# Two steps per pair for the causal convolution that is made ahead, held in place on VectorE

## The chip, the cores and the metric

The kernel runs on one core of a Trainium2 chip. The metric is the device time of one execution in microseconds (us), lower is better. Everything is float32.

## The reference, cut to what matters

A tensor `x` of 4 sequences (b) x 512 time steps (t) x 128 x 64 features passes through two layers.

Layer 0, for each sequence: a layer norm, three projections to 64 states, a decaying scan over time and a projection back ("attention"); a layer norm and a 3-tap convolution over the frequency axis with a gelu; a layer norm and a **causal depthwise convolution over time** with 3 taps, followed by another layer norm; and a feed-forward block of 64 to 256 to 64 features with a gelu. Each part is added to the residual. The part that is changed is this one:

```python
xn = layernorm(x.reshape(b, t, d), ln_time_g, ln_time_b)
to = conv_general_dilated(swap(xn), time_W, (1,), [(2, 0)], feature_group_count=d)
to = layernorm(swap(to + time_b), time_ln_g, time_ln_b)
x = x + to.reshape(b, t, f, h)
```

Layer 1 splits off a moving average over time, mixes the lowest 128 Fourier modes of the rest with complex weights, transforms back and adds the average.

## The kernel before, in words

Layer 0 holds a sequence as 64 chunks of 128 features x 512 times; two chunks are a **pair**, so that most tiles are 128 x 2 x 512. A sequence goes through five stages, each a Python generator that issues its instructions and yields after every small step: `project` (J), `scan` (Z), `attend_and_convolve` (A), `convolve_time` (C), `open_feed` (O) and `feed_forward` (F). `in_turn` runs two sequences against each other: a list of stage pairs with weights says which generator makes the next step. In two of these stretches F of sequence b (0, then 1) runs beside J and Z of sequence b+2.

The order of the instructions on TensorE is the order in which the program issues them (`manual_schedule`). On VectorE, ScalarE, GpSimd (POOL) and the DMA queue of SyncE (SP) a scheduler sorts them when the kernel is built, by program order and by when it takes them to be ready, so an instruction whose inputs are there early can be placed far ahead of its place in the program. `tc.keep_in_program_order(ins)` adds an edge from the last instruction that the program gave to the same engine: `ins` is issued after that one. It sets no upper end.

**Feed-forward** steps through c = 0 to 65. Step c issues `widen(c, 0)` and `widen(c, 1)` (four matmuls of L656 into PSUM tiles `m` and `c`, each followed by a gelu on ScalarE, L660); for odd c `add_residual` (two ScalarE instructions, L633, themselves held in program order, and the VectorE sum L636), for even c `residual` (two loads and the VectorE instructions L624 and L625); `narrow(c-1)` (eight matmul records of L667 into the single PSUM tile `p`, then the VectorE instruction L672, which empties it into `x4t`); and `store(c-2)` (four transposes, ScalarE copies, and for each fourth chunk a store of 1 MB on POOL's queue, L692). One step of `project` follows: two matmul pairs of L360, and for each pair of chunks two loads into a tile `wx` (two buffers), two VectorE scalings (L357) and two statistics (L344).

**The causal convolution** of a pair is in `taps`: a load of the pair (L555), two VectorE instructions that normalize it (L556, L557), two on ScalarE that make the first tap (L560), four on VectorE that add the other taps (L564), a correction of two columns on POOL (L568) and a store of the result to DRAM on POOL's queue (L569). `convolve_time` does this for all 32 pairs of a sequence. For sequences 1 and 2 the first 12 pairs (`AHEAD`) are made ahead by the generator `convolve_ahead`, from inside `feed_forward` of the sequence before, on tiles `x1` (three buffers) and `z` (four); `convolve_time` later fetches these results. `convolve_ahead` first spreads two rows of statistics over the partitions with matmuls into `p` (L240, copied by L284), in two calls, and then makes one pair per call. `feed_forward` calls it at the head of each step with c % 4 == 3: the rows at c = 3 and 7, the pairs at c = 11 to 55.

Of the kernel before, what the change touches and what calls it, by code (L numbers as in the profile page):

```python
# [12 lines left out]
ALU = mybir.AluOpType  # L13
# [9 lines left out]
SL = 512  # L23
# [56 lines left out]
def layer0(ctx, tc, dram, x, xt, vecs, wkvr, wo, wdec, wconv, fbias, w1, fb1, w2, fb2, x4):  # L80
# [4 lines left out]
    nc = tc.nc  # L85
# [464 lines left out]
        return t  # L550


    def taps(b, i, x2, xr, to, rb, mb):

        nc.sync.dma_start(x2, x2d[b][2 * i : 2 * i + 2].rearrange("c p t -> p c t"))  # L555
        nc.vector.tensor_tensor(xr, x2, pair_of(rb), ALU.mult)  # L556
        nc.vector.tensor_tensor(xr, xr, pair_of(mb), ALU.subtract)  # L557
        for j in range(2):
            c = slice(2 * i + j, 2 * i + j + 1)
            nc.scalar.activation(  # L560
                to[:, j, :], xr[:, j, :], AF.Identity, bias=tb_all[:, c], scale=vec[:, W2, c]
            )
            for k, w in ((1, W1), (2, W0)):
                nc.vector.scalar_tensor_tensor(  # L564
                    to[:, j, k:], xr[:, j, : SL - k], vec[:, w, c], to[:, j, k:], ALU.mult, ALU.add
                )
        cc = slice(2 * i, 2 * i + 2)
        nc.gpsimd.tensor_tensor(to[:, :, 0:2], to[:, :, 0:2], fix[:, cc, :], ALU.add)  # L568
        nc.gpsimd.dma_start(tod[b][cc].rearrange("c p t -> p c t"), to)  # L569

    def convolve_ahead(b):


        rb, mb = yield from rows(of_p, *carried[b], "rm3")
        ahead[b] = rb, mb
        for i in range(AHEAD):
            xr = spare("x1", SL)
            taps(b, i, xr, xr, spare("z", SL), rb, mb)
            yield

    def convolve_time(b):
        bank = of_a if b == B - 1 else of_p
        made = AHEAD if b in ahead else 0
        moment = carried.pop(b)
        if made:
            rb, mb = ahead.pop(b)
        else:
            rb, mb = yield from rows(bank, *moment, "rm" if b == B - 1 else "rm3")
        st = bank()
        waiting, added = [], 0  # L590
        n = NPR - made
        for k in range(n + 2):
            while waiting and waiting[0][0] == k - 2:
                add_up(st, 0, *waiting.pop(0)[1:], added == 0, added == NPR - 1)
                added += 1
            if k < n:
                if b == B - 1:

                    x2, xr, to, sq = spare("xp", SL), spare("x1", SL), spare("z", SL), two(bk, "sq")
                else:  # L600
                    x2 = bk.tile([P, 2, SL], F32, tag="kx", name="x2", bufs=3)
                    xr, to = two(bk, "kd"), bk.tile([P, 2, SL], F32, tag="k3", name="to", bufs=3)
                    sq = bk.tile([P, 2, SL], F32, tag="sq4", name="sq4", bufs=2)
                taps(b, made + k, x2, xr, to, rb, mb)
                nc.scalar.activation(sq, to, AF.Square)
                waiting.append((k, to, sq))
                i = k * made // n
                if i != (k + 1) * made // n:

                    to = fetch("kh", tod, b, i)  # L610
                    sq = bk.tile([P, 2, SL], F32, tag="mid", name="sq5", bufs=4)
                    nc.scalar.activation(sq, to, AF.Square)
                    waiting.append((k, to, sq))
            yield 7.0 * (NPR + 2) / (n + 2)
        mean, sq = yield from finish(st, bank, 4)
        causal[b] = moments(mean, sq, 4)
# [30 lines left out]
    def feed_forward(b):  # L647
        x3s = opened.pop(b)
        mids, x4s, obs = {}, {}, {}

        def widen(c, m):
            x3 = x3s[c // 2][:, c % 2, :]
            pm = c_bank() if m else two(ps_m, "m")
            for h in range(2):
                hs = slice(h * H, (h + 1) * H)
                nc.tensor.matmul(  # L656
                    pm[:, h, :], lhsT=w1_sb[hs, m * P : (m + 1) * P], rhs=x3[hs, :], start=True, stop=True
                )
            mid = mids[c, m] = bk.tile([P, 2, SL], F32, tag="mid", name="mid", bufs=4)
            nc.scalar.activation(mid, pm, AF.Gelu_apprx_tanh, bias=fb1_sb[:, m : m + 1])  # L660

        def narrow(c):
            pa = ps_p.tile([P, SL], F32, tag="p", name="pa")
            for m in range(2):
                mid = mids.pop((c, m))
                for h in range(2):
                    nc.tensor.matmul(  # L667
                        pa[h * H : (h + 1) * H, :], lhsT=w2_sb[:, m, :], rhs=mid[:, h, :],
                        start=(m == 0), stop=(m == 1),
                    )  # L670
            x4t = x4s[c] = bk.tile([P, SL], F32, tag="x4t", name="x4t", bufs=3)
            nc.vector.scalar_tensor_tensor(x4t, pa, fb2_sb, x3s[c // 2][:, c % 2, :], ALU.add, ALU.add)  # L672
            if c % 2:
                x3s.pop(c // 2)

        def store(c):
            x4t = x4s.pop(c)
            pool, tag = (ps_s, "s") if free_s[0] else (ps_p, "p")
            pt = pool.tile([P, NT, P], F32, tag=tag, name="pt")
            for t in range(NT):  # L680
                nc.tensor.transpose(pt[:, t, :], x4t[:, t * P : (t + 1) * P], ident)  # L681
            s = c // 4
            if c % 4 == 0:
                obs[s] = bk.tile([P, NT, SL], F32, tag="ob", name="ob")
            o = obs[s][:, :, c % 4 * P : (c % 4 + 1) * P]
            if c // 2 % 2:
                for h in range(2):
                    nc.scalar.copy(o[:, :, halves[1 - h]], pt[:, :, halves[h]])  # L688
            else:
                nc.scalar.copy(o, pt)  # L690
            if c % 4 == 3:
                nc.gpsimd.dma_start(  # L692
                    x4[b][:, s * SL : (s + 1) * SL].rearrange("(t p) d -> p t d", p=P), obs.pop(s)
                )

        early = None
        for c in range(NCH + 2):
            if b + 2 < B and c % 4 == 3:
                early = early or convolve_ahead(b + 1)
                next(early, None)  # L700
            if c < NCH:
                widen(c, 0)
                widen(c, 1)
            i = c // 2 + 2
            if i < NPR:
                if c % 2:
                    x3s[i] = add_residual(b, i, *coming)
                else:
                    coming = residual(b, i)
            if 0 < c <= NCH:  # L710
                narrow(c - 1)
            if c > 1:
                store(c - 2)
            yield 4.5


# [358 lines left out]
```

## Time and profile before

| what | value |
|---|---|
| median of 3 runs | 3868.74 us (3863.71 to 3873.1) |
| the profiled execution: its own time | 3868.33 us |
| the profiled execution: its span | 3866.3 us |
| TensorE (PE) busy, of the span | 3643.1 us, 94% |
| VectorE (DVE) busy | 2695.6 us, 70% |
| ScalarE (ACT) busy | 1722.6 us, 45% |
| POOL busy | 567.9 us, 15% |
| mean DMA rate | 236 GB/s |
| causal taps, L564, on tiles `z` | 224 instructions, 744 ns each (median) |

The span runs from the first to the last instruction on the core; the run's own time is 2.0 us longer. A line such as "ACT xf L871 <- PE a L867: 234.1, 64, 27.0" in a list of waits says that ScalarE stood idle ahead of L871 for 234.1 us in 64 waits, at most 27.0 us, until TensorE's L867 had finished. In a timeline a line has the start, the length, the engine, the program line, the operation and, in brackets, how long the engine was idle before it and what ended that.

The two stretches with F beside J and Z lie at about 830 to 1255 us and 1525 to 1955 us of the span.

### The profile page before, as it was taken

To read this page: it belongs to the slowest core of one execution; us is meant where nothing else is said; L and a number is where in the kernel's file an instruction comes from. 1 tells how busy PE (TensorE), PEld (TensorE's weight loads), DVE (VectorE), ACT (ScalarE), POOL (GpSimd) and SP (SyncE) were. 2 spreads that over 40 slices of the span, in tenths; PEclk is the share of its full clock that TensorE was granted. 3 is DMA by queue.
4 is the path that set the end of the run, shared out by engine and by line. 5 is a ranking of instruction groups with operands and counts; after the bars stand their busy time and mean duration, and the time that the engine had idled before them with its cause. 6 is when DMAs were issued, how large, how long until landed. Compare 5 with 4: busy or idle time off the path is not lost. (4 is left out here: it accounts for less than half of the span.)

```text
span 3866.3 us, 44881 instructions
## 1 busy us (share of the span) xinstructions
PE 3643.1 (94%) x15945; PEld 1343.5 (35%) x15945; DVE 2695.6 (70%) x3498; ACT 1722.6 (45%) x2427; POOL 567.9 (15%) x910
## 2 busy tenths in 40 slices
PE   9999999988999999899999988999989999999999
PEld 4433322233333223333322322333322843326533
DVE  4445669978656896865689799855558267792577
ACT  0023346645556564555656578867742210022100
POOL 0000012211000121110012121100025101141011
PEclk9999999999999999999999999999989999999999
DMA  9767657777765787776568677645559468994587
GB/s 310 262 215 251 222 181 260 258 242 273 255 229 183 235 279 259 248 257 231 191 229 274 215 252 248 213 162 179 182 192 289 145 217 293 314 295 157 191 299 266
DMA packets 432695, 913.86 MB, mean 236 GB/s; under 512 B 36248, under 2 KB 86616, under 8 KB 428376
## 3 DMA queue, kind: packets, MB, share of 16 engines
q1 hardware_dynamic: 350080, 634.55, 49.3%
q0 software_dynamic: 79872, 274.77, 20.3%
q8 instruction: 127, 2.08, 0.2%
q10 hardware_dynamic: 2520, 1.67, 0.1%
q14 instruction: 96, 0.79, 0.1%
HBM read 642.35 MB, written 268.50 MB: 236 GB/s over the span
## 5 line engine op out<-in xcount | busy, mean ns | idle before, releaser
L667 PE MATMUL pa<-mid,w_sb 128*64 128x512 f32 x2048 | 505.9, 615 | 74.0 <-DVE x4t L672 73.5
L660 ACT ACTIVATE mid<-m,fb_sb 128x1024 f32<-128x1024 f32 x256 | 284.5, 1111 | 245.0 <-PE m L656 244.5
L672 DVE SCALAR_TENSOR_TENSOR x4t<-pa,fb_sb,x 128x512 f32<-128x512 f32 x252 | 187.7, 745 | 200.5 <-PE pa L667 200.5
L656 PE MATMUL m<-x,w_sb 64*128 64x512 f32 x1008 | 291.7, 651 | 1.0 <-ACT mid L660 0.7
L660 ACT ACTIVATE mid<-c,fb_sb 128x1024 f32<-128x1024 f32 x256 | 283.0, 1106 | 1.2 <-PE c L656 1.1
L667 PEld LDWEIGHTS pa<-mid,w_sb 128*64 128x64 f32 x2048 | 126.3, 138 | 421.3 <-issue 223.8
L656 PE MATMUL c<-x,w_sb 64*128 64x512 f32 x1008 | 264.1, 597 | 4.7 <-ACT mid L660 4.7
L360 PE MATMUL a<-xp,wx 128*128 128x512 f32 x512 | 246.5, 608 | 6.2 <-DVE wx L357 5.7
L943 PE MATMUL b<-xin,avg_sb 128*128 128x512 f32 x512 | 230.8, 593 | 3.3 <-DVE xin L949 3.3
L949 DVE TENSOR_TENSOR xin<-b,pm 128x512 f32<-128x512 f32 x256 | 159.2, 683 | 96.4 <-PE b L946 81.5
L920 ACT COPY two<-a 128x512 f32<-128x512 f32 x64 | 37.5, 585 | 424.1 <-PE a L915 424.1
L523 ACT ACTIVATE sq<-x 128x1024 f32<-128x1024 f32 x128 | 134.9, 1054 | 200.6 <-DVE x L520 200.6
L564 DVE SCALAR_TENSOR_TENSOR to<-kd,vec,to 128x510 f32<-128x510 f32 (+1 forms) x288 | 210.7, 744 | 18.7 <-ACT to L560 16.9
L633 ACT ACTIVATE kd<-kd,vec 128x512 f32<-128x512 f32 x256 | 193.5, 809 | 7.1 <-DVE kd L625 7.1
L846 DVE TENSOR_TENSOR uv<-xin 128x1024 f32<-128x1024 f32 x128 | 156.3, 1226 | 46.9 <-PE a L860 30.1
L250 PE MATMUL st<-x,ones 128*32 128x512 f32 x512 | 173.7, 606 | 13.8 <-DVE x L520 13.5
L344 DVE BATCH_NORM_STATS2 stt<-wx 128x6 f32<-128x512 f32 x174 | 113.1, 685 | 101.2 <-DMA wx<-in_x 100.7
L825 DVE COPY xf<-b 128x256 f32<-128x256 f32 x128 | 54.4, 425 | 183.2 <-PE b L889 182.6
L681 PEld LDWEIGHTS pt<-ident,x4t 128*128 128x128 f32 x1024 | 108.3, 141 | 210.9 <-ACT mid L660 155.0
L692 POOL DMA_DIRECT2D x<-ob x64 | 49.0, 766 | 899.9 <-ACT ob L688 853.6
L357 DVE TENSOR_SCALAR wx<-wx,vec 128x192 f32<-128x192 f32 x174 | 48.8, 318 | 189.0 <-DMA wx<-in_wkvr 170.9
L482 PE MATMUL a<-rst,wo_sb 64*128 64x512 f32 x512 | 150.5, 662 | 30.8 <-DVE x L484 28.6
(238 smaller groups left out, 6803.4 us busy)
## 6 DMA issues: line engine op xcount, KB each, us to landing
xp<-in_xt SPq DMA_DIRECT2D x256, 512.0 KB
xin<-x SPq DMA_DIRECT2D x128, 1024.0 KB
kh<-to SPq DMA_DIRECT2D x152, 512.0 KB
x<-x POOLq DMA_DIRECT2D x128, 512.0 KB, 4.0
kx<-x SPq DMA_DIRECT2D x128, 512.0 KB
x<-ob POOLq DMA_DIRECT2D x64, 1024.0 KB, 6.6
out<-xin POOLq DMA_DIRECT2D x64, 1024.0 KB, 7.1
x<-x SPq DMA_DIRECT2D x96, 512.0 KB
```

The costliest lines, as they stand in the source:

```text
L250: nc.tensor.matmul(st[32 * q : 32 * q + 32, :], lhsT=ones, rhs=src[:, j, :], start=first, stop=last,)
L360: nc.tensor.matmul(pa[:, k, :], lhsT=wq[:, j, k * P : (k + 1) * P], rhs=xp[:, j, :], start=first and j == 0, stop=last and j == 1,)
L482: nc.tensor.matmul(at[:, j, :], lhsT=wo_sb[js, :], rhs=rst[js, :], start=True, stop=True)
L564: nc.vector.scalar_tensor_tensor(to[:, j, k:], xr[:, j, : SL - k], vec[:, w, c], to[:, j, k:], ALU.mult, ALU.add)
L633: tc.keep_in_program_order(nc.scalar.activation(d[:, j, :], d[:, j, :], AF.Identity, bias=vec[:, B4, c], scale=vec[:, G4, c]))
L656: nc.tensor.matmul(pm[:, h, :], lhsT=w1_sb[hs, m * P : (m + 1) * P], rhs=x3[hs, :], start=True, stop=True)
L660: nc.scalar.activation(mid, pm, AF.Gelu_apprx_tanh, bias=fb1_sb[:, m : m + 1])
L667: nc.tensor.matmul(pa[h * H : (h + 1) * H, :], lhsT=w2_sb[:, m, :], rhs=mid[:, h, :], start=(m == 0), stop=(m == 1),)
L672: nc.vector.scalar_tensor_tensor(x4t, pa, fb2_sb, x3s[c // 2][:, c % 2, :], ALU.add, ALU.add)
L846: nc.vector.tensor_tensor(t, xin[:, 0:2, :], xin[:, 2:4, :], op)
L943: nc.tensor.matmul(po[j], lhsT=avg_sb[:, j, :], rhs=xin[:, j, :], start=True, stop=False)
L949: nc.vector.tensor_tensor(by_n(xin[:, j, :]), by_n(po[j]), by_c(pm[j % 2][:, j // 2, :]), ALU.add)
```

## The change

`taps` is split into `normed` (the load and the two normalizing instructions) and `tapped` (all that follows). `convolve_time` calls both in a row, as before. `convolve_ahead` now yields between them, so that a pair takes two calls. In the pairs made ahead, the first normalizing instruction and the first VectorE tap are each held behind what the program gave VectorE before them. `feed_forward` calls the generator at the end of its step, after `store`, for each odd c above 8, in place of the head of the steps with c % 4 == 3. The rows are thus spread at c = 9 and 11, pair i is normalized at c = 13 + 4i and gets its taps at c = 15 + 4i, the last at c = 59. What VectorE was given last at these places is L672 of `narrow(c-1)`.

```diff
-    def taps(b, i, x2, xr, to, rb, mb):
+    def normed(b, i, x2, xr, rb, mb, pinned=False):
         nc.sync.dma_start(x2, x2d[b][2 * i : 2 * i + 2].rearrange("c p t -> p c t"))
-        nc.vector.tensor_tensor(xr, x2, pair_of(rb), ALU.mult)
+        first = nc.vector.tensor_tensor(xr, x2, pair_of(rb), ALU.mult)
+        if pinned:
+            tc.keep_in_program_order(first)
         nc.vector.tensor_tensor(xr, xr, pair_of(mb), ALU.subtract)
+
+    def tapped(b, i, xr, to, pinned=False):
         for j in range(2):
             c = slice(2 * i + j, 2 * i + j + 1)
             nc.scalar.activation(
                 to[:, j, :], xr[:, j, :], AF.Identity, bias=tb_all[:, c], scale=vec[:, W2, c]
             )
             for k, w in ((1, W1), (2, W0)):
-                nc.vector.scalar_tensor_tensor(
+                tap = nc.vector.scalar_tensor_tensor(
                     to[:, j, k:], xr[:, j, : SL - k], vec[:, w, c], to[:, j, k:], ALU.mult, ALU.add
                 )
+                if pinned and j == 0 and k == 1:
+                    tc.keep_in_program_order(tap)
...
         for i in range(AHEAD):
             xr = spare("x1", SL)
-            taps(b, i, xr, xr, spare("z", SL), rb, mb)
+            normed(b, i, xr, xr, rb, mb, True)
+            yield
+            tapped(b, i, xr, spare("z", SL), True)
             yield
...
-                taps(b, made + k, x2, xr, to, rb, mb)
+                normed(b, made + k, x2, xr, rb, mb)
+                tapped(b, made + k, xr, to)
...
         for c in range(NCH + 2):
-            if b + 2 < B and c % 4 == 3:
-                early = early or convolve_ahead(b + 1)
-                next(early, None)
             if c < NCH:
                 widen(c, 0)
                 widen(c, 1)
...
             if c > 1:
                 store(c - 2)
+            if b + 2 < B and c > 8 and c % 2:
+                early = early or convolve_ahead(b + 1)
+                next(early, None)
             yield 4.5
```

## The prediction

> **What bounds the kernel now.** First the page's 40 slices, for where TensorE falls short:
>
> ```profile
> PE   9999999988999999899999988999989999999999
> DVE  4445669978656896865689799855558267792577
> ```
>
> A slice is 96.7 us. Slices 10 and 17 (from zero 9 and 16) show PE at 8 and VectorE at 8, and slices around them PE at 9 and VectorE at 5 or 6. These are the heads of the two F stretches that hold the pairs made ahead. The chain that ended last reaches back only to 2262 us and is no help. So next the busy times by stretch, columns PE, PEld, DVE, ACT, POOL, clock, DMA share, GB/s:
>
> ```profile
> 880.00:1000.00 120.00, 100.80 (x386) 36.34 (x384) 104.54 (x136) 70.58 (x96) 24.22 (x28) 0.99 0.79 275
> 1000.00:1180.00 180.00, 176.71 (x696) 64.85 (x694) 102.71 (x141) 99.46 (x131) 6.54 (x9) 1.00 0.66 232
> 1577.00:1690.00 113.00, 96.52 (x358) 34.72 (x356) 100.15 (x133) 69.08 (x95) 21.99 (x28) 0.94 0.79 278
> 1700.00:1880.00 180.00, 177.87 (x699) 65.34 (x700) 101.75 (x140) 97.39 (x130) 5.37 (x8) 1.00 0.68 229
> ```
>
> VectorE is 87 to 89% busy early in each F and 57% later. The same view for L564 alone puts all 48 taps of the 12 pairs at 880 to 985 us (and 48 at 1577 to 1680 us), none later. The program asks for them over c = 11 to 55, some 270 us: the scheduler drew them forward into some 105 us. The waits of TensorE, 880:1000 and then 1000:1180:
>
> ```profile
> PE pa L667 <- DVE x4t L672: 16.7, 11, 3.0
> ...
> PE pa L667 <- DVE x4t L672: 3.3, 8, 1.1
> ```
>
> `narrow` has one PSUM tile `p`; L672 empties it, from behind taps. TensorE's timeline gives the size. A step of F with its piece of J takes 6.09 us where nothing is late (starts of L667 at 1013.61, 1019.70). From L667 at c = 7 (880.71) to c = 22 (994.61) 15 steps take 113.9 us, against 91.35: **22.5 us lost**. In the second F 1577.07 to 1690.05 loses **21.6 us**. The two spreads of rows cost too: beyond 6.09 + 0.97 (eight L240 records) the steps at c = 3 and 7 lose 0.5 and 4.6 us, in the second F 1.8 and 4.6. In all 55.6 us.
>
> Last, VectorE's timeline where nothing is ahead, because this is where the work goes:
>
> ```profile
> 1015.59 0.75 DVE L672 SCALAR_TENSOR_TENSOR x4t<-pa,fb_sb,x 128x512 f32<-128x512 f32 x1 [1.04 <-PE pa L667]
> 1016.48 1.23 DVE L636 TENSOR_TENSOR x<-kd,kx 128x1024 f32<-128x1024 f32 x1
> 1017.74 1.23 DVE L624 TENSOR_TENSOR kd<-kh,rm 128x1024 f32<-128x1024 f32 x1
> 1019.00 1.23 DVE L625 TENSOR_TENSOR kd<-kd,rm 128x1024 f32<-128x1024 f32 x1
> 1024.81 0.55 DVE L357 TENSOR_SCALAR wx<-wx,vec 128x192 f32<-128x192 f32 x2 [4.58 <-DMA wx<-in_wkvr]
> 1025.27 0.74 DVE L672 SCALAR_TENSOR_TENSOR x4t<-pa,fb_sb,x 128x512 f32<-128x512 f32 x1
> ...
> 1034.35 0.55 DVE L357 TENSOR_SCALAR wx<-wx,vec 128x192 f32<-128x192 f32 x2 [1.89 <-DMA wx<-in_wkvr]
> ```
>
> and SP's queue beside it:
>
> ```profile
> 1017.73 0.37 SPq L549 DMA_DIRECT2D kx<-x  x1
> 1018.19 0.44 SPq L337 DMA_DIRECT2D wx<-in_wkvr  x1
> ```
>
> There are holes of 4.6 and 1.9 us in turn ahead of L357. But they end a loop: L636 frees the buffer for `kx`, `wx` is queued behind `kx` on SP, L357 waits for `wx`, and an L672 is queued behind L357. It has some slack: `p` is needed one step after `narrow`, 6.09 - 1.94 - 0.75 = 3.4 us. From L636 to L357 it is 8.3 us when POOL's 1 MB store (issued at 1017.27) lands beside it, and 5.6 us from 1028.72 to 1034.35 without. With the long lag the slack is used up, with the short one some 2.7 us are left.
>
> **What the Trainium skill says.** "Perfetto Trace Analysis", Optimization Strategy: where the most-contended engine changes over time, interleaving the regimes can help. The four rows above are such regimes. "PSUM — Partial Sum Buffer", Engine vs sequencer instructions: VectorE's queue is strictly first in, first out; the L672 behind a waiting L357 agrees. "DMA: Bandwidth & Descriptors", Issuing engines are not separate DMA queues: transfers from SP and POOL interleave on the same engines; the lags of 8.3 and 5.6 us agree. "TensorE: Matmul & The Clock Gate", Part 1: idleness lowers the clock; after a wait of 3.01 us at 902 us L667's group took 2.54 instead of 1.94 us, inside the 22.5.
>
> **The change, part by part.** Instructions and bytes stay; all moves are in time and order.
>
> *The burst goes: -44.1 us.* The pins forbid it: a pair's first VectorE instruction cannot pass L672 of its step. From start to start a pair costs VectorE 2 x 1.14 (L556, L557) + 4 x 0.66 (L564) = 4.9 us. Per four steps VectorE has 0.57 x 24.4 = 13.9 us; with a pair 18.8, or 77%. By load it fits.
>
> *The rows: -11.5 us, and 2 us back.* Their old waits are behind the L672 that is stuck behind L357. At the end of an odd step the L672 concerned (that of 1015.59) has no L357 ahead: it ends 0.85 us after its matmuls, 0.49 us of which the transposes cover. I take 0.5 us for each of four; up to 3 if VectorE is late.
>
> *The halves in their new places: 14 us back.* They are released by an L672 like that at 1015.59. L636 comes earlier in the program but waits for L633, and starts 0 to 0.15 us after that L672. If it is taken as ready, it goes first and the half falls into the hole: nothing. If not, one instruction of 1.14 us (L556) or 0.66 us (a tap) goes ahead of L636, and L636 ahead of the rest. `normed` is at c % 4 == 1; chunk c-2 then fills an `ob`, so these are the halves with the store and no slack, and 1.14 us would reach TensorE; the tap's 0.66 has 2.7 us of slack. 24 pairs x 1.14 = 27.4 us at most, 0 at least. I take half, as the trace can't tell which: 14 us. Nothing below zero is excluded by an argument, but the later steps lose only 3 to 4 us in all, so a gain there is small.
>
> *The end of F: 6 us back.* c = 57 and 59 lie beside Z, where VectorE has 48.70 of 70 us (1190:1260) and TensorE waits 4.6 us for `rst`, L442, at 1226 us. 2.28 + 2.64 us join its chain, less the 2.1 us that L357 waits there: 2.8, or 3 rounded. From 0 to 5 us for each F.
>
> *Queues.* Per F, SP issues 12 loads (L555), each waiting until an `x1` is free, that is for the taps of three pairs before; in the burst this held SP for 52.7 us, with `kx` and `wx` queued behind. Now four steps lie between them. POOL's 12 corrections and 12 stores wait for taps; behind them are only the 1 MB stores, with two `ob` and 24 us for each. ScalarE's 24 L560 wait for L557, gelus queued behind; in the burst one held ScalarE for 8.2 us, which goes. I price these at zero: holes of 2 us before most gelus cover two L560 (1.5 us). Without that cover each pair could cost 1 us more.
>
> Sum: -55.6 + 2 + 14 + 6 = -33.6, say **-34 us**. The profiled execution has 3868.3 (span 3866.3 plus 2.0), 0.4 below the median: **3835 us**.
>
> **Rivals.** *The loop takes it back (slower).* A whole half goes ahead of L636, or the 512 KB load goes ahead of `wx` in SP's queue. 2.28 us for `normed`, plus half of what 1 MB did to the lag (8.3 - 5.6)/2 = 1.35: 3.6 us per pair, x 24 = 87, with 8 for rows and end 95, so +39: 3908 us; with 2.28 alone +7, 3876. It decides from (55.6 - 8)/24 = 2.0 us per pair. For it: the lag leaves no slack. Against: L636 has program order on its side, and the holes are longer than a half.
>
> *It collects elsewhere (about no change to a small gain).* A pin is only a lower end: halves may slip, and gather beside Z. If 4 of 12 pairs do, a third of the burst's 44 returns where `rst` is waited for, beyond the 22 already charged: 3850 us; with all 44, 3879.
>
> *It does nothing*: excluded for the order, since L672 itself waits for TensorE's fixed order.
>
> **Numbers.** 0.2%, 8 us, is about what a measurement tells from none. The forecast has 0.52 (its own range 3815, nothing back but the rows, to 3858); the loop 0.28, nearly all slower; collecting 0.20, half faster. Faster 0.62, same 0.10, slower 0.28. The range 3814 to 3886 leaves out the heavier end of the loop, 0.1, and more gain than all that is lost, under 0.1.
>
> **What would show it.** L564 on `z` spread from about c = 15 to 59, one pair each 24.4 us; VectorE near 75 to 80% there; 6.1 to 6.4 us from L667 to L667 through c = 8 to 53; waits L240 <- L672 under 1 us. Wrong: L636 later behind its L672 with "wx" waits later by as much, TensorE's waits for L672 spread over 48 steps at 2 us or more per pair, or the wait for `rst` longer by more than 5 us.

## The result, and the profile after

| | before | after |
|---|---|---|
| median | 3867.68 us (12 runs) | 3866.63 us (12 runs) |
| ratio of after to before | | 0.9994, 95% interval 0.9982 to 1.0006 |
| span of the profiled execution | 3866.3 us | 3870.3 us |

The change makes no difference that can be measured; a gain of 34 us was forecast. From here on line numbers are those of the changed kernel. L555 to L557 of before are L555, L556 and L559, L560 is L564, L564 is L568, L568 and L569 are L574 and L575, and the lines of the feed-forward stage are higher by 9: L636 is L645, L667 is L676, L672 is L681.

First the page's 40 slices, for TensorE and VectorE:

```profile
PE   9999999999998999998999988999989999999999
DVE  4455669966767895566789799845558267892577
```

The 8s of TensorE at slices 9, 10 and 17 are gone; the 13th (the end of the first F) and the 19th (late in the second) are now 8. The busy times by stretch, columns as before:

```profile
880.00:1000.00 120.00, 112.52 (x450) 42.22 (x448) 77.36 (x104) 66.65 (x90) 8.38 (x10) 1.00 0.69 236
1000.00:1180.00 180.00, 170.57 (x666) 62.39 (x664) 127.49 (x172) 103.69 (x140) 19.17 (x23) 0.99 0.76 262
1577.00:1690.00 113.00, 105.19 (x416) 39.18 (x414) 66.95 (x87) 63.40 (x86) 8.51 (x11) 0.98 0.68 228
1700.00:1880.00 180.00, 163.53 (x627) 59.07 (x628) 119.50 (x160) 97.38 (x132) 17.03 (x20) 0.98 0.72 240
```

The burst is gone: TensorE has 112.5 us of the first stretch where it had 100.8. It is paid for in the later stretches, 170.6 instead of 176.7 us and 163.5 instead of 177.9 us, where VectorE is 71% and 66% busy. So TensorE stands while VectorE has a third of its time free. The waits of TensorE, first from 880 to 1190 us, then from 1577 to 1895 us:

```profile
PE pa L676 <- DVE x4t L681: 16.4, 11, 2.3
```

```profile
PE pa L676 <- DVE x4t L681: 20.5, 12, 3.1
PE c L665 <- ACT mid L669: 5.6, 5, 1.1
```

It is the wait of before, for the same instruction of VectorE. Before, it stood ahead of 1000 us; now it comes once in every pair.

**A measure for each stage.** TensorE's timeline gives the start of L676 in each step c. What a step takes above 6.09 us is called its excess. In us, first F and second F:

| | before | after | change, both |
|---|---|---|---|
| from c = 1 to c = 64 | 415.0, 411.2 | 405.1, 416.8 | -4.3 |
| excess, c = 2 to 12 | 15.1, 16.8 | 5.4, 3.7 | -22.8 |
| excess, c = 13 to 22 | 14.1, 12.8 | 2.8, 6.4 | -17.7 |
| excess, c = 23 to 54 | 3.9, 2.7 | 13.1, 26.6 | +33.1 |
| c = 54 to 64, all its time | 59.2, 56.1 | 61.0, 57.4 | +3.1 |

The two stages together give back 4.3 us. The profiled execution is still 4.0 us longer in span. Its first F begins 6.6 us later (844.1 instead of 837.5 us), although the program is the same up to there. Among the kernels below, e4 apart, that start lies anywhere between 832.7 and 845.8 us. This is spread from run to run, and I explain only what lies inside the two F.

The excess of after from c = 13 to 54 is not spread evenly. In the first F 14.2 of 15.9 us are at c % 4 == 3. In the second F 17.1 are at c % 4 == 2 and 13.4 at c % 4 == 3, of 33.0. The two stages lose in different ways. VectorE, SP's queue and TensorE's L676 in the first F:

```profile
1000.04 1.94 PE L676 MATMUL pa<-mid,w_sb 128*64 128x512 f32 x8
1002.03 0.75 DVE L681 SCALAR_TENSOR_TENSOR x4t<-pa,fb_sb,x 128x512 f32<-128x512 f32 x1 [2.74 <-PE pa L676]
1002.70 1.22 DVE L556 TENSOR_TENSOR x<-x,rm 128x1024 f32<-128x1024 f32 x1
1003.83 1.22 DVE L645 TENSOR_TENSOR x<-kd,kx 128x1024 f32<-128x1024 f32 x1
1004.32 0.37 SPq L337 DMA_DIRECT2D wx<-in_wkvr  x1
...
1010.16 0.32 DVE L357 TENSOR_SCALAR wx<-wx,vec 128x192 f32<-128x192 f32 x1 [2.85 <-DMA wx<-in_wkvr]
1010.40 1.22 DVE L634 TENSOR_TENSOR kd<-kd,rm 128x1024 f32<-128x1024 f32 x1
1011.53 0.74 DVE L568 SCALAR_TENSOR_TENSOR z<-x,vec,z 128x511 f32<-128x511 f32 x1
1012.20 0.68 DVE L344 BATCH_NORM_STATS2 stt<-wx 128x6 f32<-128x512 f32 x1
1012.80 0.73 DVE L681 SCALAR_TENSOR_TENSOR x4t<-pa,fb_sb,x 128x512 f32<-128x512 f32 x1
...
1013.59 1.94 PE L676 MATMUL pa<-mid,w_sb 128*64 128x512 f32 x8 [1.29 <-DVE x4t L681]
```

The half of the next pair (L556) goes ahead of the residual's sum (L645), and the rest of the residual (L634) slips behind L357, which waits 2.85 us for `wx`. When `wx` is there, three instructions stand between L357 and the L681 that TensorE needs.

The order of SP's queue has changed too. Its longest waits from 1000 to 1180 us, first of before, then of after:

```profile
SPq L549 <- DVE x L636: 125.0, 14, 9.9
```

```profile
SPq L337 <- PE a L360: 120.0, 13, 11.4
```

Before, `wx` was queued behind the load of `kx`, which waits for the residual's sum. After, `wx` stands ahead of it and is issued at 1004.32, 0.04 us after the end of TensorE's L360, for which SP waits there. So the half ahead of the residual's sum does not make `wx` late here. Of the nine stalls at c % 4 == 3, eight have L357 10.1 to 11.0 us after the L676 of its step (10.12 above); in the lines of before that the prediction shows it was 11.20 us (1024.81 after 1013.61). What has grown is the distance from L357 to the instruction that empties `p`: 2.64 us here, 0.46 us there. The distance costs nothing where `wx` comes early: in the one pair without a stall, at c = 31, L357 starts 7.2 us after the L676.

In the second F the residual's sum goes ahead of L556 in nine of the twelve pairs, and `wx` is behind `kx` as before:

```profile
1710.68 0.36 SPq L555 DMA_DIRECT2D x<-x  x1
1711.14 0.72 POOL L575 DMA_DIRECT2D to<-z  x1 [1.14 <-issue]
...
1712.42 0.37 SPq L337 DMA_DIRECT2D wx<-in_wkvr  x1
...
1719.94 0.55 DVE L357 TENSOR_SCALAR wx<-wx,vec 128x192 f32<-128x192 f32 x2 [7.54 <-DMA wx<-in_wkvr]
1721.17 1.29 DVE L344 BATCH_NORM_STATS2 stt<-wx 128x6 f32<-128x512 f32 x2 [0.68 <-DMA wx<-in_x]
1722.37 0.73 DVE L681 SCALAR_TENSOR_TENSOR x4t<-pa,fb_sb,x 128x512 f32<-128x512 f32 x1
...
1723.16 3.30 PE L676 MATMUL pa<-mid,w_sb 128*64 128x512 f32 x8 [2.77 <-DVE x4t L681]
```

Here VectorE has nothing to do for 7.54 us. The load of a pair and the store of another, 512 KB each, are issued within 1.8 us ahead of `wx`'s weights, which are used 7.5 us after their issue. L681 is queued behind them. (The residual's two loads, 512 KB each, stand 2 to 4 us ahead of `wx` as well, as they did before.)

The L676 at 1723.16, after its wait of 2.77 us, takes 3.30 instead of 1.94 us. Three such steps, at 1694.33, 1723.16 and 1861.52, hold 4.7 of the 13.4 us at c % 4 == 3; they follow from the stalls ahead of them. The waits for L669 hold another 5.6.

### The profile page after: what moved, and what is told of

It is laid out like the page before. It is cut to its first block, busy times and chain, and to the rows that moved or that the text cites. A ratio compares the mean times of both kernels' runs of the same rounds, so it can differ in the third digit from the quotient of the medians.

```text
span 3870.3 us, 44876 instructions
## 1 busy us (share of the span) xinstructions
PE 3643.6 (94%) x15945; PEld 1343.2 (35%) x15945; DVE 2689.6 (69%) x3498; ACT 1721.7 (44%) x2427; POOL 570.3 (15%) x910
## 3 DMA queue, kind: packets, MB, share of 16 engines
q10 hardware_dynamic: 2520, 1.67, 0.1%
## 5 line engine op out<-in xcount | busy, mean ns | idle before, releaser
L676 PE MATMUL pa<-mid,w_sb 128*64 128x512 f32 x2048 | 504.7, 614 | 75.8 <-DVE x4t L681 75.8
L669 ACT ACTIVATE mid<-m,fb_sb 128x1024 f32<-128x1024 f32 x256 | 284.8, 1112 | 261.7 <-PE m L665 261.2
L681 DVE SCALAR_TENSOR_TENSOR x4t<-pa,fb_sb,x 128x512 f32<-128x512 f32 x252 | 187.5, 744 | 228.0 <-PE pa L676 228.0
L665 PE MATMUL m<-x,w_sb 64*128 64x512 f32 x1008 | 290.4, 649 | 0.2 <-DVE x L645 0.2
L669 ACT ACTIVATE mid<-c,fb_sb 128x1024 f32<-128x1024 f32 x256 | 283.0, 1105 | 1.5 <-PE c L665 1.5
L676 PEld LDWEIGHTS pa<-mid,w_sb 128*64 128x64 f32 x2048 | 125.8, 137 | 421.9 <-issue 236.1
L665 PE MATMUL c<-x,w_sb 64*128 64x512 f32 x1008 | 264.7, 598 | 7.2 <-ACT mid L669 7.2
L360 PE MATMUL a<-xp,wx 128*128 128x512 f32 x512 | 246.1, 607 | 6.3 <-DVE wx L357 5.8
L568 DVE SCALAR_TENSOR_TENSOR to<-kd,vec,to 128x510 f32<-128x510 f32 (+1 forms) x288 | 210.4, 744 | 16.0 <-ACT to L564 14.3
L250 PE MATMUL st<-x,ones 128*32 128x512 f32 x512 | 175.4, 609 | 13.3 <-DVE x L520 13.1
L880 ACT COPY xf<-a 128x512 f32<-128x512 f32 x128 | 73.5, 630 | 236.5 <-PE a L876 236.5
L521 POOL DMA_DIRECT2D x<-x x128 | 93.3, 729 | 571.0 <-DVE x L520 551.4
L357 DVE TENSOR_SCALAR wx<-wx,vec 128x192 f32<-128x192 f32 x174 | 48.9, 315 | 184.8 <-DMA wx<-in_wkvr 181.6
```

Of the source, the lines that this page charges most:

```text
L250: nc.tensor.matmul(st[32 * q : 32 * q + 32, :], lhsT=ones, rhs=src[:, j, :], start=first, stop=last,)
L360: nc.tensor.matmul(pa[:, k, :], lhsT=wq[:, j, k * P : (k + 1) * P], rhs=xp[:, j, :], start=first and j == 0, stop=last and j == 1,)
L568: tap = nc.vector.scalar_tensor_tensor(to[:, j, k:], xr[:, j, : SL - k], vec[:, w, c], to[:, j, k:], ALU.mult, ALU.add)
L665: nc.tensor.matmul(pm[:, h, :], lhsT=w1_sb[hs, m * P : (m + 1) * P], rhs=x3[hs, :], start=True, stop=True)
L676: nc.tensor.matmul(pa[h * H : (h + 1) * H, :], lhsT=w2_sb[:, m, :], rhs=mid[:, h, :], start=(m == 0), stop=(m == 1),)
```

## The experiments

The ratio is to the kernel before, measured on the same chip. The excess is that of c = 13 to 54 at the c % 4 where most of it lies. Lengths and excess are read from one profiled execution of each kernel. The seven that leave the place, the call and the step of the halves as in after have a first F between 404.6 and 408.3 us, so 3 or 4 us between two kernels say little. e4, e8, e9 and e11 stand in the text alone. "Lag" is the time from the issue of `wx`'s weights on SP to the start of L357, a mean over the second F from about 1600 to 1850 us.

| kernel | ratio, 95% interval | first F: length; c % 4 = 3 | second F: length; c % 4 = 2; 3 |
|---|---|---|---|
| before | 1 | 415.0; 6.8 | 411.2; 6.0; 3.7 |
| after | 0.9994 (0.9982 to 1.0006) | 405.1; 14.2 | 416.8; 17.1; 13.4 |
| e1 loads on POOL | 1.0013 (1.0000 to 1.0027) | 405.4; 15.9 | 421.2; 23.2; 13.3 |
| e2 call in the residual's step | 0.9969 (0.9957 to 0.9981) | 393.8; 5.5 | 417.8; 23.7; 10.3 |
| e3 both | 0.9936 (0.9918 to 0.9955) | 395.0; 5.3 | 399.7; 6.7; 5.8 |
| e5 no pins | 0.9981 (0.9972 to 0.9991) | 413.0; 9.6 | 404.2; 5.8; 5.8 |
| e6 load given earlier | 0.9999 (0.9986 to 1.0011) | 404.6; 14.5 | 414.3; 16.0; 14.6 |
| e7 load and store moved | 0.9964 (0.9952 to 0.9977) | 408.3; 18.2 | 403.0; 5.7; 11.5 |
| e12 store moved alone | 0.9962 (0.9949 to 0.9976) | 408.2; 17.8 | 400.4; 4.6; 11.5 |
| e13 L564 behind both L669 | 0.9986 (0.9972 to 1.0000) | 406.2; 14.6 | 415.4; 21.5; 9.5 |
| e14 e12 and e13 | 0.9958 (0.9942 to 0.9975) | 405.2; 17.3 | 399.9; 8.4; 4.1 |
| e15 e2 and e12 | 0.9928 (0.9909 to 0.9947) | 396.5; 8.4 | 400.5; 8.1; 4.7 |
| e10 e3 with L564 on POOL | 0.9934 (0.9919 to 0.9950) | 392.5; 4.9 | 396.4; 5.6; 6.1 |

**The queue of the load (e1).**

```diff
-        nc.sync.dma_start(x2, x2d[b][2 * i : 2 * i + 2]...)
+        (nc.gpsimd if pinned else nc.sync).dma_start(x2, x2d[b][2 * i : 2 * i + 2]...)
```

> The changed kernel with one edit: the 12 loads (L555) of the pairs made ahead are issued from POOL's queue and not from SP's. VectorE's order stays as it is; the bytes stay. Theory A (the place in SP's queue is the cause in the second F, where each of these loads stands right ahead of the loads of wx): the lag from the issue of wx to L357 falls from 7.2 to under 6 us in the half with the taps, TensorE's losses in the steps with c % 4 == 2 of the second F fall from 17 us to under 6 us; the first F, where the load stands 10 us ahead of wx, stays within 3 us. In all 10 to 17 us less than the changed kernel: 3849 to 3857 us. Rival B (it is the bytes that collide, whatever the queue): nothing moves by more than 4 us, 3863 to 3870.

Measured: 1.0013, nothing gained, and the second F is 4.4 us longer. On POOL the load is issued right behind the store and still ahead of `wx` (1699.19 the store, 1699.92 the load, 1700.43 `wx`; L357 starts at 1708.46). So it is not the place in SP's queue that makes `wx` late.

**The place of the halves (e2).** The call moves from the end of the odd steps to right behind `residual` in the even steps:

```diff
                     coming = residual(b, i)
+                    if b + 2 < B and c > 6:
+                        early = early or convolve_ahead(b + 1)
+                        next(early, None)
...
-            if b + 2 < B and c > 8 and c % 2:
-                early = early or convolve_ahead(b + 1)
-                next(early, None)
```

> The changed kernel with the call of the generator moved within the step: in even steps from c = 8, right after residual, so that each half is held behind L634 (the residual's second instruction) and not behind the L681 that empties p. Loads stay on SP. Theory A (in the first F the stall of 1.4 us per pair comes from what stands between L645 or L357 and the L681 that TensorE waits for): the first F loses its 14 us in the steps with c % 4 == 3 and is 10 to 14 us shorter; the second F keeps the load ahead of wx on SP and gains under 10 us. 3846 to 3857 us. Rival B (wx lands late whatever VectorE does, because of the bytes): the stalls stay at 1 us per pair or more, 3860 to 3872.

Measured: 0.9969. The first F falls by 11.3 us, its excess at c % 4 == 3 from 14.2 to 5.5. The second stays (417.8 us). VectorE's timeline of this kernel in the first F, with the issue of `wx` and TensorE's L676:

```profile
999.98 0.42 SPq L337 DMA_DIRECT2D wx<-in_wkvr  x1
...
1000.79 1.22 DVE L634 TENSOR_TENSOR kd<-kd,rm 128x1024 f32<-128x1024 f32 x1
...
1001.94 1.22 DVE L556 TENSOR_TENSOR x<-x,rm 128x1024 f32<-128x1024 f32 x1
...
1003.19 1.23 DVE L559 TENSOR_TENSOR x<-x,rm 128x1024 f32<-128x1024 f32 x1
1006.96 0.55 DVE L357 TENSOR_SCALAR wx<-wx,vec 128x192 f32<-128x192 f32 x2 [2.55 <-DMA wx<-in_wkvr]
1007.43 0.75 DVE L681 SCALAR_TENSOR_TENSOR x4t<-pa,fb_sb,x 128x512 f32<-128x512 f32 x1
1008.23 1.94 PE L676 MATMUL pa<-mid,w_sb 128*64 128x512 f32 x8 [0.57 <-DVE x4t L681]
```

The halves now stand in the hole ahead of L357, behind L634, and L681 follows L357 at once. L357 waits 2.55 us for `wx`, nearly as long as the 2.85 us of after, yet TensorE waits 0.57 instead of 1.29 us. Here `wx` is behind `kx` on SP again and even comes later: L357 starts 11.55 us after the L676 of its step (995.41), against 10.12 in after. So in the first F the stall is not that `wx` has become later; it is what stands between L357 and L681. The four kernels with this place (e2, e3, e10, e15) have 4.9 to 8.4 us left there; those with the changed kernel's place, call and step (after, e1, e6, e7, e12, e13, e14) 14.2 to 18.2.

**Both (e3).** The edits of e1 and e2 together.

> Both edits: the halves behind L634, and the loads of the pairs made ahead on POOL's queue. Theory A (two causes, one for each F): the gains add, both F lose under 0.5 us per pair; 25 to 40 us less than the kernel before: 3828 to 3843 us. Rival B (one cause, the lag of wx by bytes): no better than the better one of the two single edits.

Measured: 0.9936. The second F loses 18.1 us against e2, though e1 had gained nothing by the same edit. With the halves in the new place POOL comes to the store and the load later: `wx` is issued at 1713.61 us, the store at 1714.70, the load at 1715.43, and L357 starts at 1717.59, 4.0 us after the issue. That fits a cause in the bytes that go ahead of `wx`: of the 18 times that `wx` is issued between 1598 and 1853 us, 17 have no transfer of a pair made ahead in the 2.6 us before, and their mean lag is 4.30 us.

**A buffer of its own for the weights (e4).** Inputs and weights of J get tiles of their own, with three buffers for the weights; the room comes from a constant that is broadcast instead of stored.

```diff
-                both = spare("wx", 4 * S + SL)
-                wq, xk = both[:, :, 0 : 4 * S], both[:, :, 4 * S :]
+                wq, xk = fr.tile([P, 2, 4 * S], F32, tag="wq", name="wq", bufs=3), spare("wx", SL)
```

> The changed kernel with wx split into the projection's weights (wq, three buffers) and its inputs (two buffers as before); to make room, the decay row of the scan is read by a broadcast and not from a copy of 2 KB. The weights can then be loaded one pair earlier. Theory A (TensorE's stalls in both F end in L357 waiting for wx): L357's waits of 46 and 75 us all but vanish, and with them most of the 14 and 30 us of TensorE: 3825 to 3845 us. Rival B (the stalls are VectorE's own order, the halves ahead of L645 and L681): L357's waits vanish too, but TensorE keeps more than half of its stalls: 3850 to 3865 us.

Measured: 1.0051 (1.0033 to 1.0068). The second F is down to 384.8 us with 0.3 us of excess from c = 23 to 54. But the split also moves work of J into the stages before: the first F starts at 870.6 us, and the stretch between the two F grows from 279 to 302 us. The theory was that VectorE would hardly wait for the weights any more. It does, 57.0 us in the first F and 93.3 in the second, against 50.4 and 82.7 in after. VectorE's order and the transfers ahead of the weights have changed as well, so e4 does not show what makes the loss of the second F. In its first F three instructions still stand between the scaling of the weights and the one that empties `p`, and 9.0 us are left at c % 4 == 3.

**The pins (e5).** Both `keep_in_program_order` are left out.

```diff
-            normed(b, i, xr, xr, rb, mb, True)
+            normed(b, i, xr, xr, rb, mb)
             yield
-            tapped(b, i, xr, spare("z", SL), True)
+            tapped(b, i, xr, spare("z", SL))
```

> The change with both orders to the scheduler (keep_in_program_order) left out; the calls stay in the odd steps after c = 8 and each pair still comes in two calls. Theory, the pins do the spreading: without them the pieces are drawn forward again as in the kernel before, so the cost comes back into the steps just after the first call (c = 9 to 22, 15 to 35 us above 6.09 us a step in each feed-forward stage) and the steps c = 23 to 54 fall to under 5 us, from 13.1 and 26.6 in the changed kernel; time 0.997 to 1.003 of before, and the first four steps keep the gain of the row statistics. Rival, the later place and the two calls are enough: the steps c = 9 to 22 stay under 8 us and the time lies within 0.3 % of the changed kernel with its 13 and 27 us in place.

Measured: 0.9981. The burst is back: the steps c = 13 to 22 have 18.2 and 17.3 us of excess, the steps 23 to 54 only 7.5 and 3.4. The same view as for the changed kernel, VectorE's busy time in L568 alone in the first two stretches, first of this kernel and then of after:

```profile
880.00:1000.00 120.00, 28.38 (x40) 0.97 0.77 266
1000.00:1180.00 180.00, 6.08 (x9) 1.00 0.68 237
```

```profile
880.00:1000.00 120.00, 8.91 (x12) 1.00 0.69 236
1000.00:1180.00 180.00, 20.79 (x28) 0.99 0.76 262
```

The pins do the spreading, and it is the spread halves that cost in c = 23 to 54. Without them the later start alone keeps its gain at c = 2 to 12, and the kernel is at least as fast as the changed one (the two intervals overlap).

**Load and store apart (e6, e7, e12).** In e6 the load of the next pair is pinned in the call of `normed`; in e12 the correction and the store of a pair are pinned in the next pair's first call; e7 has both.

```diff
+        coming = get(0)                     # e6, e7: get() is the load, pinned on SP
         for i in range(AHEAD):
-            xr = spare("x1", SL)
+            xr = coming                     # e6, e7
             normed(b, i, xr, xr, rb, mb, True)
+            coming = get(i + 1) if i + 1 < AHEAD else None   # e6, e7
+            if i:                           # e7, e12: put() is correction and store
+                put(b, i - 1, to, True)
             yield
```

> In the changed kernel the 512 KB load of the next pair is issued in the call that does the taps' step, beside the 512 KB store of the pair finished; here it is pinned on SP in the other call, with the residual's half, so load and store lie two steps apart. VectorE's order is the same. Theory A, two transfers together ahead of wx's weights make the second stage's stall: the stage from 1528 to 1945 us loses most of the 17.1 us at c % 4 == 2 (under 8 left) and the lag from wx's issue to its first use falls from 7.5 to about 5 us; some of it may come up in the other half of the pair; the first stage, where load and wx stand otherwise, within 4 us of 405. Time 0.9965 to 0.9990 of before. Theory B, it is the pieces on VectorE ahead of L344 and L357 that make the stall in both stages: no change, second stage 413 to 421 us, time 0.998 to 1.001.

Measured in e6: 0.9999. The edit did not part the two on the chip, since SP runs ahead of the other engines: in the second F the load is issued at 1703.38, the store at 1703.85 and `wx` at 1704.97 us. So e6 says nothing on the theory.

> As the run before, with the correction and the store of a pair moved to the same later call too, so that load and store are together again, two steps later than in the changed kernel. VectorE's order is the same. Theory A, bytes together ahead of wx: the stall of the second stage moves with them, from c % 4 == 2 (17.1 us) to c % 4 == 0 or 1 of the same size, or stays where it was if the halves on VectorE decide; time 0.999 to 1.002 of before. Theory B, the pieces on VectorE: the stall stays at c % 4 == 2 and 3 with 13 to 20 us each.

Measured in e7: 0.9964, better than either theory had it. The load is still ahead of `wx` (1705.47, `wx` 1706.91), but the store now comes behind it (1713.70). The stall at c % 4 == 2 falls from 17.1 to 5.7 us and does not come up elsewhere. This pointed to the store alone.

> The changed kernel with the correction and the store of a pair moved to the next pair's first call, two steps later, pinned on POOL; loads and VectorE's order as in the changed kernel. Theory, the lag of wx follows the bytes issued in the 2.6 us ahead of it (second stage: 4.2 us with none, 5.1 with one transfer of 512 KB, 6.8 with two): the store leaves, the load stays, so the lag at the half with the load goes from 6.8 to about 5 us and the second stage's 17.1 us at c % 4 == 2 to 4 to 9 us; c % 4 == 3 (ScalarE) stays at 10 to 15; second stage 402 to 408 us, time 0.996 to 0.998 of before. Rival, the load alone is enough to make it late: c % 4 == 2 stays at 14 us or more, time 0.999 to 1.001.

Measured in e12: 0.9962, as the theory had it; the second F falls from 416.8 to 400.4 us, just below the 402 to 408 expected; the first, 408.2, lies at the upper end of the spread named above. VectorE's order, the load and its queue are those of after. The same stretch of the second F (L692 is this kernel's L681, L687 its L676):

```profile
1701.20 0.36 SPq L555 DMA_DIRECT2D x<-x  x1
...
1702.42 0.37 SPq L337 DMA_DIRECT2D wx<-in_wkvr  x1
...
1708.06 0.68 DVE L357 TENSOR_SCALAR wx<-wx,vec 128x192 f32<-128x192 f32 x2 [5.14 <-DMA wx<-in_wkvr]
...
1709.22 0.72 POOL L581 DMA_DIRECT2D to<-z  x1 [0.30 <-POOL z L578]
...
1710.86 0.73 DVE L692 SCALAR_TENSOR_TENSOR x4t<-pa,fb_sb,x 128x512 f32<-128x512 f32 x1
...
1711.65 1.94 PE L687 MATMUL pa<-mid,w_sb 128*64 128x512 f32 x8 [1.25 <-DVE x4t L692]
```

With the store gone from ahead of `wx` the wait of L357 is 5.14 instead of 7.54 us, and TensorE's 1.25 instead of 2.77 us. The lag by how many transfers of pairs made ahead (the load of one, the store of another) were issued in the 2.6 us ahead of `wx`, or with it, second F. The residual's loads and the 1 MB stores are not counted; the former stand ahead of `wx` in nearly every step.

| of pairs made ahead | kernel: mean lag in us (number of steps) |
|---|---|
| nothing | after 4.21 (10), e12 4.30 (12), e14 4.64 (12), before 4.14 (17); in the other kernels 4.06 to 4.87 |
| one transfer of 512 KB | e12 4.87 (7), e7 5.06 (8), e15 4.96 (8), e14 5.44 (8) |
| two | after 6.81 (8), e6 6.80 (7), e13 7.37 (8), e1 7.59 (6), e2 5.99 (8) |

In the first row L357 is often not waiting for `wx` at all but for its turn on VectorE, so the differences between the rows are not times of a transfer. The step from none to one is small, and its lower end lies in the range of the first row; that to two is clear. e2 has the smallest lag of the last row and yet 23.7 us of excess, so the mean lag does not give the loss alone; its greatest single lag, 9.1 us, is the greatest of that row.

**ScalarE (e9, e13, e14).** In the changed kernel L564 stands between the two L669 of a step and waits for L559, with the second L669 behind it. e9 puts L564 on POOL:

```diff
-            nc.scalar.activation(to[:, j, :], xr[:, j, :], AF.Identity, bias=tb_all[:, c], scale=vec[:, W2, c])
+            nc.gpsimd.tensor_scalar(to[:, j, :], xr[:, j, :], vec[:, W2, c], tb_all[:, c], ALU.mult, ALU.add)
```

> The changed kernel with L564 of the pairs made ahead (z <- x, scale and bias) on POOL instead of ScalarE, 24 instructions of 128x512 in each feed-forward stage; nothing else. In the changed kernel's planned order L564 stands between the two L669 of a step, and waits there for L559 on VectorE (6.97 us at 1727.73), with the second L669 behind it. Theory, this queue on ScalarE makes the second stage's 13.4 us at c % 4 == 3 (1.40 us in each pair, two L564 of 0.7 us): under 5 us left there, while the 17.1 us at c % 4 == 2 (wx late behind the store and the load) stay at 14 to 22; second stage 402 to 409 us; the first stage's 14.2 at c % 4 == 3, which is L681 behind L357 and pieces on VectorE, stays at 10 to 17. Time 0.996 to 0.999 of before. Rival, the two halves on VectorE ahead of L681 make the stall at c % 4 == 3 in the second stage too: it stays at 11 to 17 there, time 0.999 to 1.002.

Measured: 1.0016 (1.0006 to 1.0026). It tells nothing on ScalarE. Two taps now stand ahead of L681 in the second F, and they wait for L564: a pair's two take 2.3 to 3.4 us on POOL there, where one takes 0.8 us on ScalarE; the excess at c % 4 == 3 rises to 29.6 us. e13 gives the two L564 pinned behind both L669, and VectorE's order in the second F is untouched:

```diff
                 widen(c, 1)
+            if early and c % 4 == 2 and 13 < c < 61:
+                next(early, None)           # issues the two L564, each pinned
```

> The changed kernel with the two L564 of a pair given right after the next step's L665 and L669, pinned on ScalarE behind them; the call comes in c % 4 == 2. The planned order of ScalarE goes from L669 L564 L669 L564 to L669 L669 L564 L564 in both stages; VectorE's order in the second stage is the same, in the first two stt go ahead of a tap. Theory, the second L669 queued behind L564 makes the second stage's 13.4 us at c % 4 == 3: under 4 us left there, c % 4 == 2 stays at 13 to 20, second stage 402 to 408 us; first stage's 14.2 at c % 4 == 3 within 4 us of it, since there L681 is behind L357 and pieces on VectorE. Time 0.996 to 0.999 of before. Rival, the two halves of L556 and L559 on VectorE ahead of L681 make it: c % 4 == 3 stays at 10 us or more in the second stage, time 0.9985 to 1.001.

> The same with the correction and the store two steps later as well (that alone gave 0.9962). Theory, the losses add: second stage 388 to 394 us with under 6 us at each c % 4, first stage 400 to 410 us, time 0.992 to 0.995 of before. Rival, the slack that one repair leaves is taken by the other wait: second stage 397 to 402 us, time 0.9955 to 0.997.

Measured: e13 0.9986, e14 0.9958. In e13 the excess at c % 4 == 3 falls from 13.4 to 9.5 us, but that at c % 4 == 2 rises from 17.1 to 21.5: the sum stays. On top of the later store it is the same, 11.5 to 4.1 and 4.6 to 8.4, and the second F has 399.9 instead of 400.4 us. The waits of L665 for L669 are gone in both, 5.6 us of them in after. In e13 four groups of L676 take 2.7 to 3.5 us instead, after waits of 2.1 to 2.9 us. My theory fell, and the rival of e14 held: what L564 ahead of L669 costs, another wait takes when it is gone.

> The version with the call between residual's two steps and the ahead loads on POOL (0.9936 of before) with L564 on POOL as well; VectorE's order is the same as in that run. Theory: what is left there at c % 4 == 3 in the second stage, 5.8 us, and part of the first stage's 5.3 is L564 on ScalarE, behind the two L669 but ahead of ob's copies; it goes to under 3 us each, second stage 393 to 398 us, first 391 to 395; time 0.990 to 0.993. Rival: L564 behind both L669 does no harm any more, and POOL's longer L564 makes the taps later: 0.993 to 0.996.

Measured in e10: 0.9934 against 0.9936 without the move of L564, the same. The two F, 392.5 and 396.4 us, are as long as the theory had them, but the excess at c % 4 == 3 that it was to remove is still there, 4.9 and 6.1 us.

**Even steps (e8, e11).** The call in even steps, `c % 2 == 0` for `c % 2`; e11 has L564 on POOL too.

> The changed kernel with the call in the even steps (c = 10, 12, ...) where the changed kernel has it in the odd ones; nothing else. The planned order then puts both instructions of a half behind the step's last L672-type write of x4t (L681 here), ahead of wx's inputs, and in the second stage the load goes right behind xp and not right ahead of wx's weights. Theory A (in stage one, what stands on VectorE between wx's inputs and L681; in stage two, bytes just ahead of wx): stage one about 394 to 400 us (under 6 us at any c % 4), stage two 400 to 410 us; time 0.993 to 0.998 of before. Rival, an even step is no better since VectorE has the same work between two L681: both stages within 4 us of the changed kernel's 405 and 417, time 0.998 to 1.001.

> The kernel with the call in even steps (time 0.9996 of before; stages 422.2 and 399.0 us) with L564 on POOL. Theory: the 17.5 us that its first stage loses at c % 4 == 0, 1.6 us each, are L564 on ScalarE ahead of L669 (TensorE's L665 waits for mid L669 at 991.80 and 993.50); they go to under 5 us, first stage 400 to 411 us, second 395 to 400; time 0.993 to 0.997. Rival: VectorE's halves make them: first stage within 4 us of 422, time 0.998 to 1.001.

Measured: e8 0.9996 (0.9987 to 1.0005), e11 1.0019 (1.0009 to 1.0028). In e8 the second F is 399.0 us, just below what the theory expected; there the store and the load come behind `wx` (1723.17 and 1722.78 against 1721.21). The first F misses by far: 422.2 us, longer than before, with a mean lag of `wx` of 7.4 us (930 to 1180 us). In e11 17.5 us at c % 4 == 0 become 10.8, but 9.5 at c % 4 == 3 become 20.6. What binds the first F in this version was not found.

**The two repairs together (e15).** The call of e2 and the store of e12.

> The version with the call between residual's two steps (L564 behind both L669; time 0.9969; second stage 417.8 us with 23.7 at c % 4 == 2) with the correction and the store of a pair in the next pair's first call; loads stay on SP ahead of wx. Theory, in the second stage only the store's bytes were in the way: c % 4 == 2 under 8 us, second stage 392 to 400 us, first stage 392 to 397; time 0.990 to 0.994 of before, which is the prediction's 0.9914 (3835 of 3868). Rival, the load alone keeps wx late: second stage over 406 us, time 0.995 to 0.997.

Measured: 0.9928 (0.9909 to 0.9947), or 28 us of 3872, the fastest of all. First F 396.5, second 400.5 us, at the upper end of what was expected or just past it. It cannot be told from e3 and e10, which get there by another way. Against e2 only the store has moved, and the second F falls from 417.8 to 400.5: the second pair of kernels, beside after and e12, that shows the price of the store, 17.3 and 16.4 us.

## Why the prediction was wrong

**What bounds the kernel: right.** TensorE waited for L672 behind the burst, and the burst went. The four stretches show it.

**The burst and the rows: right.** They were to give 53.6 us after the 2 us for the rows. The steps c = 2 to 22 lost 58.8 us before; after, c = 2 to 12 lose 9.1. With the stalls from c = 13 on counted below, 49.7 us came back. The waits of L240, priced at 0.5 us for each of four, are 0.5 us for two in each F.

**The halves in their new places: the step that failed.** They were priced at 14 us, half of 24 x 1.14. The steps c = 13 to 54 have 15.9 and 33.0 us of excess, 48.9 in all; less the 6.6 us that before had at c = 23 to 54, the term is 42.3 us, three times its size. With it, the three terms give -49.7 + 42.3 + 3.1 = -4.3 us. Two things were wrong in it.

In the first F the prediction asked whether L636 or the half goes first, leant on program order, and took the mean. The trace shows the half ahead (1002.70 before 1003.83), but it does not cost by the path that was priced. That path led from L636 over `kx` and `wx` to L357, with the L672 right behind. On SP `wx` no longer waits behind `kx`, and L357 is not later than before. What was not priced is the order behind L357: with the halves ahead of it, the residual's L634 and a tap come after it and ahead of L681. The 14.2 us are nine stalls, 1.37 to 1.67 us each but for one of 2.41. That this is near the upper end of the prediction, 12 x 1.14, is chance. The experiments e2, e3, e10 and e15 take most of it away by another place, e2 with L357 later than in after.

In the second F L636 does go ahead of the half in nine of twelve pairs, the case priced at nothing. The 33.0 us are 2.75 us for each pair, and about half of them belong to a term that was set to zero, **the queues**. "I price these at zero" weighed how long SP and POOL are held and who is queued there. Not weighed was when the bytes go: the store was counted as harmless because behind it on POOL are only other stores. It delays `wx`, which stands in another queue. Moving it gave 16.4 us, 15.1 of them in these steps. "DMA: Bandwidth & Descriptors" of the Trainium skill, Issuing engines are not separate DMA queues, was cited in the prediction for just this, and e1 agrees with it: with the load on POOL's queue the mean lag of `wx` is 7.59 us, with the load on SP's 6.81. The prediction used it for the 1 MB store of before, and for the load in a rival, but priced nothing for the two transfers that it moved itself.

**The end of F: right in kind.** 6 us were expected, 3.1 measured; the waits for `rst` are 5.3 and 3.2 us, where before they were 4.6 and 3.6.

**ScalarE at zero: right,** by e13, e14 and e10, although the trace shows L669 waiting behind L564.

**The rivals.** "The loop takes it back" came nearest, with its point of decision at 2.0 us a pair; the 48.9 us over 24 pairs are 2.04. It named L556 ahead of the residual's sum and a transfer ahead of `wx`. Both are seen, but the first costs by the order behind L357 and not by the loop, and of the transfers it had the load and not the store. It was weighed at 0.28 because "the holes are longer than a half". They are, in the mean, but a half in the hole pushed other work to the far side of it, ahead of what TensorE waits for. VectorE at 77% was the wrong comfort: it is at 71 and 66%, and TensorE waits for it. "It collects elsewhere" did not come: L568 has 28 instructions between 1000 and 1180 us.

Still open: what makes the last 11 to 13 us of excess at c = 23 to 54 in the second F of e3, e12, e14 and e15. In e12 and e14 a load still goes ahead of `wx`, but in e3 it does not.

## What to carry to other kernels

An idle stretch of an engine that ends with a wait is room only as long as the work put into it pushes nothing else behind the wait. Count what stands, after the change, between the waiting instruction and the one that the busiest engine needs next; here that distance, and not the wait, made the stall of the first F. When a step is moved, ask of each of its transfers what small load is issued in the next 2 us, on whatever queue, and who waits for that. And when one repair moves a wait from one step to its neighbour at the same sum, as e13 did, it was not on the path that binds.

## What the runs showed of the hardware

In the second F a load of 256 KB is used 4.2 us after its issue in the mean of after when no transfer of a pair made ahead goes just before it, and 6.8 us after it when two of 512 KB do; without one of the two, the store, e12 has 4.9 us. From which queue the load comes makes it no better (e1, 7.6 us). Where the transfers come 1 to 2 us behind it instead, the one step read in e3 shows 4.0 us. The busy share of the DMA engines, 0.72 in this stretch against 0.68 before, gives little sign of it.

After waits of 1.96 to 2.77 us three groups of eight L676 took 2.77 to 3.30 us instead of 1.94; after a wait of 2.00 us (at 1751.00) another still took 1.94.

For a pair's two L564 of 128x512 POOL took 2.3 to 3.4 us (e9, second F); ScalarE took 0.8 us for one.
